# A differential-attention and mixture-of-experts kernel: another order of work within a round, one further GpSimd step per round, and two norms from one set of statistics

## The chip, the cores and the metric

The kernel runs on one core of a Trainium2 chip. A core has five engines with a queue each: TensorE (PE, matmuls; its weight loads are listed apart as PEld), VectorE (DVE), ScalarE (ACT), GpSimd (POOL) and SyncE (SP), which here only issues DMAs. An engine takes its instructions in the order in which they were recorded; between engines there are semaphores. The metric is the time of one execution on the device, in microseconds, as the median of several runs.

## What is computed

One transformer layer on x of 8 sequences, 512 tokens, 128 features (float32). Attention with 16 heads of 8 features subtracts two softmaxes, and the result is normalised by the sum of its absolute values; a layer norm of the residual sum follows. Then each token goes through a second norm with gamma and beta, a router chooses two of eight experts, and the weighted outputs are added and normed again.

```python
attn = softmax(causal(q @ k1.T * SCALE)) - sigmoid(lambda_logit) * softmax(causal(q @ k2.T * SCALE))
attn = attn / maximum(sum(abs(attn)), 1e-6)
x  = layernorm(x + (attn @ v) @ Wo.T)                    # no gamma, no beta
xn = (x - mean(x)) * rsqrt(var(x) + 1e-5) * gamma + beta
w, idx = top_k(softmax((xn @ router_w.T) / 1.5), 2)      # of 8 experts
y  = sum over the two chosen e of w_e * (silu(xn @ W1[e]) @ W2[e])      # 128 -> 512 -> 128
out = layernorm(x + y)
```

## The kernel before

**Tiles.** Queries are taken in 16 units per sequence (class Unit), 32 queries each, with all 16 heads: four heads times 32 queries fill the 128 partitions, and four groups of heads (NG = 4) lie side by side. Unit j needs L = 32 (j + 1) keys. Four units are a block of 128 tokens; there are 4 blocks in a sequence and 32 in all.

**Rounds.** The attention is a pipeline of 384 rounds (function round_of). A unit with L up to 256 has two slots, each with two head groups and both softmaxes; a longer one has four slots, each with two head groups and one softmax. A slot passes through these steps, one engine each:

- scores (PE, L343 and, with the causal mask, L352), into PSUM tile sc, of which there are two buffers
- maxima (DVE, L365 for short units, L373 for long ones), into nm
- exps (ACT, L383), from sc and nm into the unit's tile et, with row sums
- combine (DVE, L395 to L399 once a unit and L409; then POOL, L419), which multiplies the second softmax's numerators in place by -c2; a unit has two pieces (short) or four (long)
- transposes (PE, L437), which turn and subtract both softmaxes of a piece in PSUM tile pt, of which there is one buffer
- evacuate (ACT, L457 and L459), from pt into aT
- times_v (PE, L469), once a unit, into po

Within one call of round_of the order of every engine is the order in which the function records its steps; nothing rearranges it. Before, a call records: times_v of the units that are ready, with the first steps of a finished block; scores of the next slot; evacuate of the pieces that the previous round transposed; the ScalarE steps that the previous round left in a list (on_act); maxima of the present slot; transposes of the pieces that the previous round combined; the VectorE steps left in a list (on_dve); combine; exps of the present slot; late VectorE steps (on_dve_late). Then come one step of a finished block or of the next sequence's projections (misc), one step of routing, one or two DMA steps on GpSimd (moves, gathers), and up to two expert steps as a budget (level, due) allows.

**Around the attention.** block_tasks has seven steps for a finished block: reciprocals, normalise, project_out, first_norm, second_norm, turn, logits; each norm has bn_stats, bn_aggr, an addition of eps on DVE and a power of -0.5 on GpSimd (L112). projection_tasks makes the next sequence's qb (queries spread over four heads by four GpSimd instructions, L292), kT and vt. The 30 first blocks form four chunks of 6, 9, 9 and 6, whose tokens are sorted by expert: route_tasks counts and places them, the queue moves sends rows to DRAM by indirect DMAs on GpSimd (L751), sparse_tasks runs tiles of 128 rows through their expert (turn: L860, L869; hidden: L889; silu: ACT L827 and DVE L829), and the queue gathers fetches rows back (L914). The last two blocks go through all experts (dense_tasks). When the attention is over, round_of is called without a slot until all lists are empty.

## Time and profile before

| what | us |
|---|---|
| median of 3 runs | 1285.85 |
| lowest, highest | 1284.31, 1290.01 |
| the profiled execution, on the device | 1278.93 |
| its span, first to last instruction | 1277.1 |
| mean granted PE clock in it | 0.926 |

The busiest groups of instructions, from the page:

| group | count | busy us | mean ns |
|---|---|---|---|
| transposes (PE, L437) | 2560 | 393.2 | 294 |
| exps, long units (ACT, L383) | 512 | 299.3 | 591 |
| multiplication (POOL, L419) | 512 | 267.7 | 528 |
| combine (DVE, L409) | 512 | 264.0 | 516 |
| maxima, long units (DVE, L373) | 256 | 251.8 | 984 |
| scores, long units (PE, L343) | 1024 | 248.7 | 562 |
| evacuate (ACT, L457) | 336 | 149.3 | 444 |
| power -0.5 (POOL, L112) | 96 | 62.1 | 647 |

A busy time is the union of a group's instructions, so that matmuls that overlap count once; a mean is the length of one. A wait is the idle time of an engine ahead of an instruction, put down to what released it. The granted clock is a share of full speed[...].

### The profile page before, as it was taken

Reading aid. Unit: us, or ns where it says so; the run is one execution under the profiler, and the core shown is the slowest. Engines: PE = TensorE matmul, PEld = TensorE weight load, DVE = VectorE, ACT = ScalarE, POOL = GpSimd, SP = SyncE. Lnnn points to the kernel's source line nnn. Section 1 sums busy time; section 2 is a strip of 40 time slices with the busy share of each in tenths; the row PEclk is TensorE's granted clock in tenths of the full one; section 3 lists DMA queues with packets and bytes.
Section 4 is the critical chain, followed back from the end, with each engine's and each line's share of the span. In section 5 each row is a group of like instructions: output and inputs, shape, how many; then the busy total and the mean of one; then the engine's idle time right before and its main releaser. Section 6 shows DMA issues by size and latency. Waiting matters only on the chain.

```text
span 1277.1 us, 30618 instructions
## 1 busy us (share of the span) xinstructions
PE 1152.4 (90%) x10538; PEld 844.4 (66%) x10538; DVE 947.2 (74%) x2900; ACT 804.3 (63%) x2912; POOL 502.6 (39%) x867
## 2 busy tenths in 40 slices
PE   5999999889999999998999999998998699879776
PEld 3666666567666766675657776785667587657665
DVE  3588768877887878986796888688777776747656
ACT  3677767666786767776656767775665465636321
POOL 3243334452423333366373332324546531244343
PEclk8599969897999999999889999999899798979998
DMA  8000000021100310020212321141023334223762
GB/s 236 1 2 2 10 1 2 26 73 51 41 22 22 92 43 22 11 83 26 61 48 69 93 63 42 43 113 48 26 72 87 111 107 114 79 66 112 224 184 66
DMA packets 115594, 82.87 MB, mean 65 GB/s; under 512 B 9584, under 2 KB 100976, under 8 KB 115440
## 3 DMA queue, kind: packets, MB, share of 16 engines
q1 hardware_dynamic: 97632, 66.67, 18.3%
q0 software_dynamic: 3840, 7.87, 2.1%
q10 hardware_dynamic: 13968, 6.37, 1.8%
q8 instruction: 85, 1.39, 0.5%
q14 instruction: 69, 0.57, 0.2%
HBM read 63.31 MB, written 17.56 MB: 63 GB/s over the span
## 4 chain that ended last, share of the span: by engine, by line
PE 64%; DVE 17%; ACT 7%; POOL 6%; issue 5%; DMA 2%; ACTq 0%; SPq 0%; POOLq 0%; DVEq 0%
PE pt L437 21%; PE sc L343 13%; PE sc_None L343 6%; PE po L469 6%; PE pa L869 5%; PE pz L889 4%; ACT et L383 4%; DVE junk L409 3%; DVE nm L373 3%; PE pmo L520 2%; DVE hT L829 1%; DVE x L924 1%; POOL l_rs L112 1%; DVE nm L365 1%; POOL et L419 1%
## 5 line engine op out<-in xcount | busy, mean ns | idle before, releaser
L419 POOL TENSOR_SCALAR et<-et,c 128x224 f32<-128x224 f32 (+15 forms) x512 | 267.7, 528 | 491.6 <-DVE junk L409 349.0
L437 PE MATMUL pt<-ident,et 128*128 128x128 f32 (+3 forms) x2560 | 393.2, 294 | 48.3 <-POOL et L419 32.4
L437 PEld LDWEIGHTS pt<-ident,et 128*128 128x128 f32 (+3 forms) x2560 | 277.6, 138 | 170.5 <-issue 45.0
L383 ACT ACTIVATE et<-sc,nm 128x512 f32<-128x512 f32 (+7 forms) x512 | 299.3, 591 | 45.0 <-DVE nm L373 31.7
L373 DVE TENSOR_REDUCE nm<-sc 128x2 f32<-128x576 f32 (+7 forms) x256 | 251.8, 984 | 60.8 <-PE sc L352 59.8
L409 DVE SCALAR_TENSOR_TENSOR junk<-et,c 128x224 f32<-128x224 f32 (+15 forms) x512 | 264.0, 516 | 9.6
L343 PE MATMUL sc<-kT,qb 32*128 32x384 f32 (+7 forms) x1024 | 248.7, 562 | 6.4 <-ACT et L383 5.6
L457 ACT COPY aT<-pt 128x256 f32<-128x256 f32 (+1 forms) x336 | 149.3, 444 | 152.7 <-PE pt L437 149.0
L383 ACT ACTIVATE et<-sc_None,nm 128x256 f32<-128x256 f32 (+7 forms) x512 | 187.2, 378 | 28.4 <-DVE nm L365 13.7
L343 PE MATMUL sc_None<-kT,qb 32*128 32x128 f32 (+7 forms) x1024 | 134.4, 377 | 9.7 <-ACT et L383 9.1
L343 PEld LDWEIGHTS sc<-kT,qb 32*128 32x128 f32 x1024 | 78.9, 188 | 61.3 <-issue 25.5
L365 DVE TENSOR_REDUCE nm<-sc_None 128x4 f32<-128x256 f32 (+7 forms) x128 | 95.8, 749 | 29.7 <-PE sc_None L352 29.5
L343 PEld LDWEIGHTS sc_None<-kT,qb 32*128 32x128 f32 x1024 | 86.0, 208 | 43.5 <-ACT et L383 16.7
L112 POOL TENSOR_TENSOR l_rs<-l_ve,nhalf 128x1 f32<-128x1 f32 x96 | 62.1, 647 | 125.0 <-DVE l_ve L110 99.5
L469 PE MATMUL po<-aT,vt 128*32 128x128 f32 (+3 forms) x2560 | 107.9, 288 | 0.0
L889 PE MATMUL pz<-xgT,w 128*128 128x128 f32 x704 | 99.9, 288 | 6.8 <-DVE xgT L863 3.6
L869 PE MATMUL pa<-w,hT 128*128 128x128 f32 x704 | 98.2, 285 | 7.0 <-DVE hT L829 4.3
L383 ACT ACTIVATION_READ_ACCUMULATOR et<-sc_None,nm 128x1 f32 x512 | 104.2, 203 | 0.0
L383 ACT ACTIVATION_READ_ACCUMULATOR et<-sc,nm 128x1 f32 x512 | 102.0, 199 | 0.0
L869 PEld LDWEIGHTS pa<-w,hT 128*128 128x128 f32 x704 | 91.2, 202 | 9.4 <-DVE hT L829 6.7
L889 PEld LDWEIGHTS pz<-xgT,w 128*128 128x128 f32 x704 | 91.4, 202 | 8.9 <-DVE xgT L863 4.3
L459 ACT COPY aT<-pt 32x128 f32<-32x128 f32 (+5 forms) x288 | 84.6, 294 | 7.6 <-PE pt L437 7.6
(143 smaller groups left out, 1290.3 us busy)
## 6 DMA issues: line engine op xcount, KB each, us to landing
w<-in_w_dram SPq DMA_DIRECT2D x192, 256.0 KB, 3.0
xg<-xs SPq DMA_DIRECT2D x88, 64.0 KB, 3.3
ys<-ysb ACTq DMA_DIRECT2D x88, 64.0 KB, 1.6
xs<-zero SPq DMA_DIRECT2D x2, 1600.0 KB, 13.4
xs<-zero SPq DMA_DIRECT2D x2, 1216.0 KB
xt<-in_x_dram SPq DMA_DIRECT2D x8, 256.0 KB, 2.9
out_dram<-ot SPq DMA_DIRECT2D x32, 64.0 KB, 1.5
xs<-xh,row POOLq DMA_INDIRECT x60, 2.3
```

The lines of the kernel that those rows point to most:

```text
L343: nc.tensor.matmul(sc[:, gi, lo : lo + L], lhsT=qb[r, j].rearrange("p h q -> p (h q)"), rhs=kT[r, si, :L], start=True, stop=False,)
L365: nc.vector.tensor_reduce(self.nm[:, g, :], sc.rearrange("p g (s l) -> p g s l", s=2)[:, :, :, : self.L], AX.X, ALU.max, negate=True,)
L373: nc.vector.tensor_reduce(self.nm[:, g, s], sc[:, :, : self.L], AX.X, ALU.max, negate=True)
L383: nc.scalar.activation(self.et[:, g, si, : self.L], sc[:, gi, lo : lo + self.L], AF.Exp, bias=self.nm[:, g, si : si + 1], accum_out=self.b ...
L409: nc.vector.scalar_tensor_tensor(junk[:, :L], self.et[:, g, 1, :L], self.c2[:, g : g + 1], self.et[:, g, 0, :L], ALU.mult, ALU.max, accum_ ...
L419: nc.gpsimd.tensor_scalar(self.et[:, g, 1, :L], self.et[:, g, 1, :L], self.c2[:, g : g + 1], -1.0, ALU.mult, ALU.mult,)
L437: nc.tensor.matmul(pt[:kw, x_ * self.n + kb, :], lhsT=self.et[:, g, k, kb * P : kb * P + kw], rhs=ident, is_transpose=True, start=(k == 0) ...
L457: nc.scalar.copy(self.aT[:, g, :full, :], src[:, :, :full, :])
L459: nc.scalar.copy(self.aT[: w[-1], g, full, :], src[: w[-1], :, full, :])
L469: nc.tensor.matmul(self.blk["po"][32 * g : 32 * g + 32, self.jj, :], lhsT=vt[:kw, kb, 32 * g : 32 * g + 32], rhs=self.aT[:kw, g, kb, :], s ...
L869: nc.tensor.matmul(pm[:, 1, :], lhsT=hT[y][:, f, :], rhs=w[y][1][:, f, :], start=(f == 0), stop=(f == NF - 1),)
L889: nc.tensor.matmul(pz[:, f, :], lhsT=w[t][0][:, f * P : (f + 1) * P], rhs=xgT[t], start=True, stop=True,)
```

## The change

round_of records its steps in another order. At the start it sets aside the pieces that are to be transposed and the units that are to be multiplied with v. Then: scores of the next slot, maxima of the present slot, combine, on_act, exps, on_dve, on_dve_late; then misc, **or** a step of routing if misc is empty; GpSimd's step; experts; and at the end evacuate of what the previous round transposed, times_v, and the transposes.

GpSimd's step is taken from a new list on_pool first, which holds the four spreads of the queries one by one; then from moves; then from gathers, but these only in a round that had neither misc nor routing.

The two norms become one step. The second norm normalises what the first one put out, so its mean is 0 and its variance v / (v + eps); from the first norm's variance v, residual makes v + eps and v (1 + eps) + eps^2, takes both to the power -0.5 in one GpSimd instruction, and norms writes xh and x1, both from xa. Three small tiles that outlast their chunk's routing (w1st, w2nd, row) get a third buffer.

```diff
@@ -286,17 +286,19 @@
                 pm = ps_m.tile([P, T], F32, tag="pm", name=f"pmq_{b}")
                 nc.tensor.matmul(pm, lhsT=wq_sb, rhs=xTf, start=True, stop=True)
 
+                def spread_head(h):
+                    nc.gpsimd.tensor_scalar(
+                        qb[:, :, h, :],
+                        qs.rearrange("p (j q) -> p j q", q=Q),
+                        hms[:, h : h + 1],
+                        1.0,
+                        ALU.mult,
+                        ALU.mult,
+                    )
+
                 def spread():
                     nc.vector.tensor_copy(qs, pm)
-                    for h in range(4):
-                        nc.gpsimd.tensor_scalar(
-                            qb[:, :, h, :],
-                            qs.rearrange("p (j q) -> p j q", q=Q),
-                            hms[:, h : h + 1],
-                            1.0,
-                            ALU.mult,
-                            ALU.mult,
-                        )
+                    on_pool.extend(lambda h=h: spread_head(h) for h in range(4))
 
                 on_dve.append(spread)
 
@@ -530,31 +532,36 @@
                     nc.vector.tensor_add(xa, pm, xts[b][:, i, :])
                     mv = bp.tile([P, 1, 2], F32, tag="mv1", name=f"mv1_{n}")
                     stats_of(bp, xa, mv[:, 0, :], "l1")
-                    s["xa"], s["mv"], s["rs"] = xa, mv, rstd_of(bp, mv, 1, "l1")
+
+
+
+                    ve = bp.tile([P, 2], F32, tag="l1_ve", name=f"l1_ve_{n}")
+                    nc.vector.tensor_scalar(ve[:, 0:1], mv[:, 0, 1:2], EPS, None, ALU.add)
+                    nc.vector.tensor_scalar(
+                        ve[:, 1:2], mv[:, 0, 1:2], 1.0 + EPS, EPS * EPS, ALU.mult, ALU.add
+                    )
+                    rs = bp.tile([P, 2], F32, tag="l1_rs", name=f"l1_rs_{n}")
+                    nc.gpsimd.tensor_tensor(rs, ve, nhalf[:, :2], ALU.pow)
+                    s["xa"], s["mv"], s["rs"] = xa, mv, rs
 
                 on_dve.append(residual)
 
-            def first_norm():
+            def norms():
                 def norm():
-                    x1 = s["x1"] = ch.x1[:, ci, :]
-                    nc.vector.tensor_scalar(
-                        x1, s["xa"], s["mv"][:, 0, 0:1], s["rs"], ALU.subtract, ALU.mult
-                    )
-                    mv = bp.tile([P, 1, 2], F32, tag="mv2", name=f"mv2_{n}")
-                    stats_of(bp, x1, mv[:, 0, :], "l2")
-                    s["mv2"], s["rs2"] = mv, rstd_of(bp, mv, 1, "l2")
-
-                on_dve.append(norm)
-
-            def second_norm():
-                def norm():
+                    x1 = ch.x1[:, ci, :]
                     if ch.sparse:
                         s["xh"] = ch.xh[:, ci, :]
                     else:
                         s["xh"] = bp.tile([P, D], F32, tag="xh", name=f"xh_{n}")
-                    nc.vector.tensor_scalar(
-                        s["xh"], s["x1"], s["mv2"][:, 0, 0:1], s["rs2"], ALU.subtract, ALU.mult
-                    )
+                    for k, dst in enumerate((s["xh"], x1)):
+                        nc.vector.tensor_scalar(
+                            dst,
+                            s["xa"],
+                            s["mv"][:, 0, 0:1],
+                            s["rs"][:, 1 - k : 2 - k],
+                            ALU.subtract,
+                            ALU.mult,
+                        )
 
                 on_dve.append(norm)
 
@@ -574,7 +581,7 @@
                 nc.tensor.matmul(pm, lhsT=s["xnT"], rhs=rw_sb, start=True, stop=True)
                 on_dve.append(lambda: nc.vector.tensor_copy(lg[:, ci, :], pm))
 
-            return [reciprocals, normalise, project_out, first_norm, second_norm, turn, logits]
+            return [reciprocals, normalise, project_out, norms, turn, logits]
 
         def route_tasks(ch):
 
@@ -648,8 +655,8 @@
                         nc.vector.tensor_mul(e2, r["ex"], r["oh2"])
                         m = small("s2")
                         nc.vector.tensor_reduce(m, e2, AX.X, ALU.add)
-                        ch.w = [r["rc"], cp.tile([P, CB], F32, tag="w2nd", name=f"w2nd_{n0}")[:, :nb]]
-                        ch.w[0] = cp.tile([P, CB], F32, tag="w1st", name=f"w1st_{n0}")[:, :nb]
+                        ch.w = [r["rc"], x1p.tile([P, CB], F32, tag="w2nd", name=f"w2nd_{n0}")[:, :nb]]
+                        ch.w[0] = x1p.tile([P, CB], F32, tag="w1st", name=f"w1st_{n0}")[:, :nb]
                         nc.vector.tensor_copy(ch.w[0], r["rc"])
                         nc.vector.tensor_mul(ch.w[1], m, r["rc"])
                     else:
@@ -722,7 +729,7 @@
                         pk = wide(f"p{k}")
                         nc.vector.tensor_mul(pk, at, r[f"oh{k + 1}"])
                         nc.vector.tensor_reduce(pos[:, k], pk, AX.X, ALU.add)
-                    ch.row = cp.tile([P, 2, CB], U32, tag="row", name=f"row_{n0}")
+                    ch.row = x1p.tile([P, 2, CB], U32, tag="row", name=f"row_{n0}")
                     nc.vector.tensor_copy(ch.row[:, :, :nb], pos)
 
                 on_dve.append(step)
@@ -1020,7 +1027,7 @@
             return tasks + [lambda c=c: on_dve.append(lambda: last[c][1]()) for c in range(nb)]
 
 
-        on_act, on_dve, on_dve_late = [], [], []
+        on_act, on_dve, on_dve_late, on_pool = [], [], [], deque()
 
         def pause():
             pass
@@ -1035,6 +1042,7 @@
             task()
             run(on_dve)
             run(on_act)
+            run(on_pool)
 
         misc, routing, experts, moves, gathers = (deque() for _ in range(5))
         to_combine, to_transpose, to_evacuate, to_multiply = deque(), deque(), deque(), deque()
@@ -1076,46 +1084,44 @@
 
 
             nonlocal due, now_at
-            for _ in range(len(to_multiply)):
-                after_blocks(to_multiply.popleft())
+            to_turn, to_times = list(to_transpose), list(to_multiply)
+            to_transpose.clear()
+            to_multiply.clear()
             if ahead:
                 ahead["sc"] = ahead["u"].scores(ahead["slot"])
-            for _ in range(len(to_evacuate)):
-                v, piece, pt = to_evacuate.popleft()
-                v.evacuate(piece, pt)
-                if piece[-1] == NG - 1:
-                    to_multiply.append(v)
-            run(on_act)
             if now:
                 now["u"].maxima(now["slot"], now["sc"])
-            for _ in range(len(to_transpose)):
-                v, piece = to_transpose.popleft()
-                to_evacuate.append((v, piece, v.transposes(piece)))
-            run(on_dve)
             left = now["left"] if now else 2
             for _ in range(-(-len(to_combine) // left)):
                 v, piece = to_combine.popleft()
                 v.combine(piece)
                 to_transpose.append((v, piece))
+            run(on_act)
             if now:
                 now["u"].exps(now["slot"], now["sc"])
                 if now["left"] == 1:
                     to_combine.extend((now["u"], piece) for piece in now["u"].pieces)
+            run(on_dve)
             run(on_dve_late)
-            room = 2
+            room, busy = 2, True
             if misc:
                 misc.popleft()()
                 room -= 1
-            if routing:
+            elif routing:
                 step = routing.popleft()
                 step()
                 room -= step.__name__ == "counts"
+            else:
+                busy = False
+
 
 
             for _ in range(1 if now and now["u"].b < B - 1 else 2):
-                if moves:
+                if on_pool:
+                    on_pool.popleft()()
+                elif moves:
                     moves.popleft()()
-                elif gathers and (now or not misc and not routing):
+                elif gathers and not busy:
                     gathers.popleft()()
             if now:
                 t, c = rounds[now_at]
@@ -1128,6 +1134,15 @@
                 due -= 1
                 room -= 1
             due = min(due, 4.0)
+            for _ in range(len(to_evacuate)):
+                v, piece, pt = to_evacuate.popleft()
+                v.evacuate(piece, pt)
+                if piece[-1] == NG - 1:
+                    to_multiply.append(v)
+            for v in to_times:
+                after_blocks(v)
+            for v, piece in to_turn:
+                to_evacuate.append((v, piece, v.transposes(piece)))
 
...
@@ -1163,7 +1178,7 @@
             attention_done = True
             while (
                 to_combine or to_transpose or to_evacuate or to_multiply
-                or misc or routing or experts or moves or gathers or on_act or on_dve or on_dve_late
+                or misc or routing or experts or moves or gathers or on_act or on_dve or on_dve_late or on_pool
             ):
                 round_of()
```

## The prediction

> **What bounds the kernel now.** I read the page's engine line and its chain of waits first, then PE's waits between 40 and 1165 us (attention without its start and drain), then one quiet stretch of the timeline, then the granted clock by windows of 10 us.
>
> ```profile
> PE 1152.4 (90%) x10538; PEld 844.4 (66%) x10538; DVE 947.2 (74%) x2900; ACT 804.3 (63%) x2912; POOL 502.6 (39%) x867
> PE 64%; DVE 17%; ACT 7%; POOL 6%; issue 5%; DMA 2%; ACTq 0%; SPq 0%; POOLq 0%; DVEq 0%
> ```
>
> TensorE is busy 90% and is 64% of the chain; 125 us of the span are left for it to be idle, and about 60 of these lie in the start and the drain. What it waits for in between:
>
> ```profile
> PE pt L437 <- POOL et L419: 32.4, 24, 4.4
> PE pt L437 <- ACT aT L457: 9.9, 14, 0.8
> PE sc_None L343 <- ACT et L383: 7.2, 17, 1.1
> PE pa L860 <- DVE hT L829: 7.1, 9, 3.8
> PE sc L343 <- ACT et L383: 5.6, 15, 0.9
> ```
>
> (waiting instruction, releaser, us in total, times, longest). The transposes wait 32.4 us for GpSimd's multiplication. The new order bears most on this. Now a round with nothing but attention in it, L = 416:
>
> ```profile
> 102.20 0.97 PE L343 MATMUL sc<-kT,qb 32*128 32x416 f32 x4
> 103.01 0.18 PE L352 MATMUL sc<-mk,i 32*128 32x32 bf16 x2
> 103.12 0.87 PE L437 MATMUL pt<-ident,et 128*128 128x128 f32 x6
> 103.37 1.02 DVE L373 TENSOR_REDUCE nm<-sc 128x2 f32<-128x832 f32 x1
> 104.03 0.37 ACT L457 COPY aT<-pt 128x256 f32<-128x256 f32 x1
> 104.30 0.27 ACT L459 COPY aT<-pt 96x128 f32<-96x128 f32 x1
> 104.46 0.61 ACT L383 ACTIVATE et<-sc,nm 128x416 f32<-128x416 f32 x1
> 105.05 0.60 ACT L383 ACTIVATE et<-sc,nm 128x416 f32<-128x416 f32 x1
> ```
>
> (start, duration). PE goes from scores to transposes to the next scores (103.97) without a gap: 1.77 us a round. ScalarE evacuates pt **before** this round's exponentials, so pt is free when the next transposes come. Last, the clock:
>
> ```profile
> 100.00:110.00 10.00, 9.96 (x89) 5.94 (x86) 8.42 (x19) 8.43 (x28) 2.90 (x5) 1.00 0.01 2
> 160.00:170.00 10.00, 9.29 (x59) 6.90 (x59) 7.54 (x30) 6.38 (x31) 3.65 (x9) 0.53 0.01 2
> 170.00:180.00 10.00, 10.00 (x57) 6.92 (x58) 5.45 (x19) 6.16 (x26) 2.47 (x5) 0.50 0.00 0
> 300.00:310.00 10.00, 9.60 (x62) 7.01 (x56) 7.48 (x28) 5.29 (x24) 3.42 (x9) 0.53 0.19 61
> 1180.00:1190.00 10.00, 6.67 (x63) 6.17 (x65) 6.62 (x23) 2.43 (x6) 6.79 (x8) 1.00 0.63 181
> ```
>
> (after the length: busy us of PE, weight load, DVE, ACT, POOL, then the granted clock.) The mean clock of 0.926 is (1 - 0.926) x 2 x 1277 = 189 us at half speed, in stretches of 5 to 30 us. PE is then saturated, so up to 94 us are lost there.
>
> **The change, part by part.**
>
> *Transposes to the end of PE's round.* They get the time of the misc and expert matmuls (about 1 us where there are any) as slack for GpSimd, and the multiplication itself is issued earlier, since combine now stands ahead of on_dve. The waits of 1.15 to 1.32 us at L = 320 (80, 204, 238, 339, 468 us) should go: 6 us. Of the other 26 (3.1 and 4.4 us at 1114 and 1125, where two sends a round keep GpSimd for some 5 us, which stays so) I take half. Sum **-19**.
>
> *Exponentials ahead of the evacuation on ScalarE.* Scores wait for them 7.2 + 5.6 us now: **-13**. But pt has one buffer. In the changed instruction order the scores wait for VectorE alone, and the transposes carry the wait for ScalarE: transposes of round r need the evacuation of r-1, which now stands behind exps of r, which need maxima of r, which need scores of r, which stand behind the transposes of r-2. That is a loop over two rounds. From the rows above: scores 0.99, maxima 1.02, exps 2 x 0.61, evacuation 0.55 (mean of one copy of 0.48 and two of 0.63), transposes 0.87, three hand-overs of about 0.06: 4.84 us for two rounds, 9.7 for a unit of four. Measured now: 7.8 (100.38 to 108.20). So PE must wait 1.9 us in this unit. The same sum for L = 352, 384, 448, 480, 512 gives 9.1, 9.5, 10.1, 10.9, 11.3; the first batch has 8.7, 7.8, 9.2, 10.4, 9.7. With 416 it falls short by 7.0 us. Over the eight batches, from the starts of the scores: 7.0, 3.5, 5.4, 4.6, 3.5, 2.3, 0.5, 0: **+27**. This is a lower end, since matmuls of one round don't fill the wait of another, and a tanh that waits for its matmuls delays exps in the loop (1.06 + 0.60 in place of 1.02): 0 to 30, I take **+15**. Units up to L = 256 take 6 to 10 us and stay above their loop.
>
> *DVE and ScalarE steps behind the attention's.* on_dve waits for the previous round's matmuls, which now come before transposes, so it stalls less; what hides it is the slack of a round. PE's expert waits (7.1, and 5.6 in smaller rows) fall by **-4**. If on_dve is late, maxima of the next round queue behind it, as now.
>
> *Norms.* Per block a stats, an aggregate and a pow go (295 + 182 ns on DVE, 647 on GpSimd), one DVE add of about 154 comes: 32 x 0.32 = 10 us of DVE, 21 us of GpSimd, beside PE's work nearly everywhere: 0 to -10, I take **-2**. Where DVE is not the bound it buys nothing. The pow on two columns costs as the one does now, within 0.1 us: nothing on the path.
>
> *One thing a round on GpSimd; misc or routing.* The four head spreads (733 ns each, 2.9 us in a row at 598.61) are parted over four rounds, counted above in the first 6 us. They go ahead of sends; the queries have over ten rounds until used. Gathers keep off rounds with misc or routing. Routing of the third chunk's count moves from round 303 to 319, so its experts begin later and 58 instead of 56 expert steps are left behind the last scores; the drain takes 108 us for 56: **+4**. Weight loads on SP go with these steps, in the same order. The row and weight tiles with a third buffer cost nothing and free nothing that was waited for.
>
> *The clock.* Stretches at half clock follow stalls on GpSimd at 240, 467, 600, 657, 884, 934, 1005 and 1113, together some 118 us, at a loss of up to 59. With the waits partly gone I take **-25** (0 to -50). Against it stand the new waits. [...] the widest gap ahead of the half clock at 160 was 0.94 us, ahead of 300 1.12, and of ten single gaps of 0.9 to 1.5 us about half are followed by it. At 1180 the clock is full with PE busy only 67%, so idleness alone doesn't decide. [...] Then scores, 51% of a plain round now (0.92 of 1.77), fall to 38% (of 2.42), near the 34% of the rounds before 160 (0.95 of 2.8). A plain round at half clock is about 3.7 us instead of 2.4 (3.9 and 4.5 measured at 662, L = 512). Some 30 units are plain, 120 rounds; none cold is 0, half 78, a quarter **+40**, which I take[...].
>
> Sum: -19 -13 +27 +15 -4 -2 +4 -25 +40 = **+23**. The profiled execution took 1278.9, its span 1277.1: 1302. The median shown is 7 us above it; I say **1304**.
>
> **Rivals.** (1) *Faster*: waits on GpSimd and their half clock go as hoped, no new half clock, the loop costs its lower end alone: -63 + 27 + 4 = -32, **1247**. For it speaks that the plain loss is small; against it, that PE would have to stay warm with a gap in each plain round. It decides once the extra of the loop and new half clock stay under 32 us. (2) *Worse*: PE is cold in most plain rounds and the old half-clock stretches remain: +23 + 38 + 25 = **1365**. For it: 160 and 300, cold with PE busy 93% and more; against it, that cold PE is saturated[...]. (3) *Cancelling*: 15 us of new half clock instead of 40 gives about **1281 to 1290**, within what can be told. (4) The order isn't what it says, because a queue or a buffer undoes it: the built order shows transposes behind the experts and combine right after maxima, so this falls.
>
> **How the numbers follow.** Slower by the loop and some half clock 0.42, cold throughout 0.14, cancelling 0.13, faster 0.31. Faster and slower by 0.5% are below 1279.4 and above 1292.3, about what a measurement tells from no change. So 0.31, 0.13, 0.56. The range 1240 to 1372 leaves a tenth at each end; the likeliest case alone is 1293 to 1340.
>
> **What would show it.** Right: PE's transposes wait for aT (evacuation) some 40 us or more instead of 13; hardly any wait of scores for et; plain units at 416 take near 9.7 us; mean clock not above 0.92. Wrong: those units still 7.8 us, or a clock of 0.95 and more with GpSimd's waits gone.

## The result, and the profile after

| what | before | after |
|---|---|---|
| median, us | 1285.08 | 1367.07 |
| lowest, highest | 1283.67, 1290.01 | 1366.49, 1378.36 |
| profiled execution, us | 1278.93 | 1366.49 |
| mean granted PE clock | 0.926 | 0.892 |

The ratio is 1.065 (95% interval 1.059 to 1.071): **slower**, by 82 us in the medians and 88 in the profiled executions, where the prediction had 23. The sign is as forecast and the time lies in the range, but it is the time of rival 2 (1365), which had been given a chance of 0.14. Here and below, medians are over all executions and ratios over the fast ones alone.

The engine line and the chain that ended last, from the page of the changed kernel:

```profile
PE 1220.1 (89%) x10538; PEld 867.5 (64%) x10538; DVE 943.3 (69%) x2836; ACT 796.5 (58%) x2912; POOL 482.8 (35%) x835
PE 61%; DVE 21%; ACT 8%; issue 4%; DMA 3%; POOL 2%; SPq 0%; ACTq 0%; POOLq 0%; DVEq 0%
```

TensorE has exactly as many matmuls as before (10538) and is busy 68 us longer with them; its idle time in the span goes from 125 to 145 us. GpSimd's share of the chain falls from 6% to 2%, and VectorE's rises from 17% to 21%: the wait that the change aims at is nearly gone from the chain, and another has come. The attention's stage alone, from 40 us to just behind its last scores, in one window of each kernel (from:to, length, then the busy us of PE, weight load, DVE, ACT and POOL, the granted clock, the DMAs' share, GB/s). Before:

```profile
40.00:1166.00 1126.00, 1047.35 (x9734) 755.51 (x9733) 863.33 (x2626) 757.05 (x2774) 446.58 (x721) 0.93 0.18 51
```

After:

```profile
40.00:1247.00 1207.00, 1108.38 (x9682) 772.78 (x9674) 854.51 (x2547) 747.88 (x2767) 422.94 (x684) 0.89 0.16 47
```

This stage has 81 of the 88 us: 61 are busy time, 20 are idle time (78.6 to 98.6). (52 fewer matmuls fall into the stage than before, and 45 more behind it.) The other engines do less than before. So the loss is mostly a slower TensorE, not a TensorE that waits longer. Its waits in that stage, by releaser, in the changed kernel:

```profile
PE pt L439 <- ACT aT L461: 34.3, 48, 1.9
PE pt L439 <- ACT aT L459: 22.7, 25, 1.4
PE pmo L522 <- DVE on L512: 7.8, 18, 1.6
...
PE pmn L570 <- DVE xh L557: 3.1, 6, 1.0
PE pt L439 <- POOL et L421: 2.4, 1, 2.4
```

(L439, L459, L461 and L421 are the transposes, the two evacuations and GpSimd's multiplication.) The transposes' wait for GpSimd has gone from 32.4 to 2.4 us, that of the scores for the exponentials from 12.8 to nothing, and in their place the transposes wait 57.0 us for the evacuation. This is the loop through the single buffer pt. One turn of it in a plain round, on the timeline:

```profile
542.21 0.57 ACT L385 ACTIVATE et<-sc,nm 128x384 f32<-128x384 f32 x1
...
542.77 0.37 ACT L459 COPY aT<-pt 128x256 f32<-128x256 f32 x1
...
543.02 0.26 ACT L461 COPY aT<-pt 64x128 f32<-64x128 f32 x1
...
543.34 0.87 PE L439 MATMUL pt<-ident,et 128*128 128x128 f32 x6 [0.94 <-ACT aT L461]
```

ScalarE finishes the exponentials, then empties pt, and only then do the transposes start, after TensorE has been idle for 0.94 us. What such a gap can be followed by shows a few rounds later:

```profile
552.53 0.87 PE L439 MATMUL pt<-ident,et 128*128 128x128 f32 x6 [1.13 <-ACT aT L461]
553.33 0.97 PE L345 MATMUL sc<-kT,qb 32*128 32x416 f32 x4
...
554.42 1.54 PE L439 MATMUL pt<-ident,et 128*128 128x128 f32 x6
```

The same six transposes take 0.87 us at 552.53, behind a gap of 1.13 us, and 1.54 us in the next round. In the first sequence the windows show how long that lasts:

```profile
100.00:110.00 10.00, 9.09 (x50) 5.14 (x50) 4.91 (x14) 6.03 (x23) 2.19 (x4) 0.69 0.01 2
110.00:120.00 10.00, 10.00 (x59) 5.89 (x58) 4.99 (x12) 4.37 (x15) 1.38 (x3) 0.50 0.00 0
```

Before, the first of these windows had 89 matmuls at a clock of 1.00; now it has 50 at 0.69, and the second runs wholly at half clock with TensorE busy all of it. In the traces of both kernels the clock is either 1 or 0.5, so half speed rules for (1 - 0.892) x 2 x 1364.8 = 295 us of the span, against 189 before.

How full TensorE is ahead of such a stretch can be counted. In the traces of both kernels all changes of the clock lie on one grid of 3.41 us: its stretches between two changes last from 3.41 to 201.39 us, each a whole multiple of 3.413. These are two neighbouring pieces of the grid, around the rounds above:

```profile
550.94:554.35 3.41, 2.25 (x18) 1.05 (x14) 2.18 (x6) 3.23 (x12) 1.17 (x2) 0.99 0.00 0
554.35:557.77 3.42, 3.35 (x13) 1.97 (x13) 1.62 (x4) 1.67 (x6) 0.58 (x1) 0.50 0.00 0
```

TensorE is busy 2.25 of the 3.41 us (66%), and the next piece is at half clock. Over both kernels, of the pieces at full clock in which TensorE is busy less than half of the time, 17 of 20 are followed by half clock; of those with one half to three quarters, 24 of 76; of those with 80% or more, 2 of 503. In the piece from 550.94 the single wait of 1.13 us is nearly all of TensorE's idle time (1.16 us).

### The profile page after: what moved, and what is told of

Read it like the earlier page. It is cut to its first block, busy times and chain, and to the rows that moved or that the text cites. A ratio compares the mean times of both kernels' runs of the same rounds, so it can differ in the third digit from the quotient of the medians.

```text
span 1364.8 us, 30258 instructions
## 1 busy us (share of the span) xinstructions
PE 1220.1 (89%) x10538; PEld 867.5 (64%) x10538; DVE 943.3 (69%) x2836; ACT 796.5 (58%) x2912; POOL 482.8 (35%) x835
## 4 chain that ended last, share of the span: by engine, by line
PE 61%; DVE 21%; ACT 8%; issue 4%; DMA 3%; POOL 2%; SPq 0%; ACTq 0%; POOLq 0%; DVEq 0%
PE pt L439 18%; PE sc L345 12%; PE po L471 7%; PE sc_None L345 6%; DVE nm L375 6%; ACT et L385 5%; PE pz L896 5%; DVE junk L411 5%; PE pa L876 4%; PE pmo L522 3%; ACT aT L459 1%; DMA got<-ys,row 1%; DVE nm L367 1%; PE pmk L307 1%; DVE x L931 1%
## 5 line engine op out<-in xcount | busy, mean ns | idle before, releaser
L421 POOL TENSOR_SCALAR et<-et,c 128x224 f32<-128x224 f32 (+15 forms) x512 | 270.4, 533 | 710.3 <-DVE junk L411 488.2
L439 PE MATMUL pt<-ident,et 128*128 128x128 f32 (+3 forms) x2560 | 402.8, 302 | 63.5 <-ACT aT L461 34.8
L439 PEld LDWEIGHTS pt<-ident,et 128*128 128x128 f32 (+3 forms) x2560 | 301.9, 145 | 148.7 <-ACT aT L461 73.4
L411 DVE SCALAR_TENSOR_TENSOR junk<-et,c 128x224 f32<-128x224 f32 (+15 forms) x512 | 258.9, 506 | 9.6
L345 PE MATMUL sc<-kT,qb 32*128 32x384 f32 (+7 forms) x1024 | 265.0, 596 | 0.0
L459 ACT COPY aT<-pt 128x256 f32<-128x256 f32 (+1 forms) x336 | 149.6, 445 | 47.3 <-PE pt L439 46.5
L345 PEld LDWEIGHTS sc<-kT,qb 32*128 32x128 f32 x1024 | 83.7, 200 | 59.9 <-issue 43.1
L471 PE MATMUL po<-aT,vt 128*32 128x128 f32 (+3 forms) x2560 | 117.3, 308 | 0.0
L896 PE MATMUL pz<-xgT,w 128*128 128x128 f32 x704 | 106.6, 299 | 5.0 <-DVE xgT L870 5.0
L834 ACT ACTIVATE th<-pz 128x512 f32<-128x512 f32 x88 | 52.7, 599 | 84.7 <-PE pz L896 83.9
L471 PEld LDWEIGHTS po<-aT,vt 128*32 128x32 f32 (+3 forms) x2560 | 66.0, 118 | 43.0 <-issue 33.5
```

The lines of the kernel that those rows point to most:

```text
L345: nc.tensor.matmul(sc[:, gi, lo : lo + L], lhsT=qb[r, j].rearrange("p h q -> p (h q)"), rhs=kT[r, si, :L], start=True, stop=False,)
L411: nc.vector.scalar_tensor_tensor(junk[:, :L], self.et[:, g, 1, :L], self.c2[:, g : g + 1], self.et[:, g, 0, :L], ALU.mult, ALU.max, accum_ ...
L421: nc.gpsimd.tensor_scalar(self.et[:, g, 1, :L], self.et[:, g, 1, :L], self.c2[:, g : g + 1], -1.0, ALU.mult, ALU.mult,)
L439: nc.tensor.matmul(pt[:kw, x_ * self.n + kb, :], lhsT=self.et[:, g, k, kb * P : kb * P + kw], rhs=ident, is_transpose=True, start=(k == 0) ...
L459: nc.scalar.copy(self.aT[:, g, :full, :], src[:, :, :full, :])
L471: nc.tensor.matmul(self.blk["po"][32 * g : 32 * g + 32, self.jj, :], lhsT=vt[:kw, kb, 32 * g : 32 * g + 32], rhs=self.aT[:kw, g, kb, :], s ...
```

## Experiments

Four theories were set against each other. **L**: the loop through pt (exponentials ahead of the evacuation) makes the waits, and the waits make the half clock. **P**: the loss comes from TensorE's new order, with the transposes behind the round's other matmuls. **V** (called D in the first expectations): VectorE's steps of on_dve come too late behind the combine and hold up the matmuls of misc and experts. **R**: it comes from the rules (one thing a round on GpSimd, misc or routing, gathers in empty rounds), which push work later. The kernel before was timed beside each run; ratios are to it, with 95% intervals.

### The changed kernel with the evacuation put back ahead

```diff
+            for _ in range(len(to_evacuate)):
+                v, piece, pt = to_evacuate.popleft()
+                v.evacuate(piece, pt)
...
             run(on_act)
             if now:
```

(and the same lines taken away at the end of round_of).

> The changed kernel with one thing put back: the evacuation of pt stands ahead of on_act and of the exponentials on ScalarE, as before the change; all else is the new order. Theory L (the loop exps, evacuation, transposes, scores, maxima over one pt buffer makes TensorE wait in each plain round, and these waits bring the half clock): the waits of the transposes for aT fall from 58 us to 20 or less, a plain unit at L = 416 goes from 9.5 us and more to 8.3 or less, the mean clock rises to 0.92 or more, and the time is 1215 to 1290 us. Rival R (the parted GpSimd steps, misc or routing, the late gathers and the later experts leave TensorE with too little work in places): the time stays above 1340 us and the clock below 0.90. Rival D (late on_dve steps hold up what follows): above 1320 us with waits for xgT, on, hT in place of those for aT.

Measured: 1357.37 us, ratio 1.058 (1.051 to 1.065). The loop is gone, the shortest units at L = 384, 416, 448 and 512 are back at 8.0, 7.9, 8.4 and 9.8 us, and the time has hardly moved. TensorE's waits in the stage (40 to 1241 us):

```profile
PE sc L345 <- ACT et L385: 16.2, 26, 1.8
PE pmo L522 <- DVE on L512: 15.8, 19, 2.6
PE pmn L570 <- DVE xh L557: 12.1, 15, 1.2
PE sc_None L345 <- ACT et L385: 10.6, 22, 1.1
PE pmc L683 <- DVE r_bothb L676: 10.4, 4, 4.1
```

Theory L alone falls, and the waits for `on` at a time above 1320 us are what theory V (rival D) had forecast. Instead of the transposes, the matmuls of the finished blocks wait now (pmo, pmn) and so do the scores. Why pmo waits is plain on the timeline:

```profile
94.48 0.55 DVE L411 SCALAR_TENSOR_TENSOR junk<-et,c 128x320 f32<-128x320 f32 x1
...
94.96 0.68 DVE L512 TENSOR_TENSOR on<-oraw,pmr 128x512 f32<-128x512 f32 x1
...
95.70 1.16 PE L522 MATMUL pmo<-wo_sb,on 128*128 128x128 f32 x8 [0.49 <-DVE on L512]
```

VectorE takes the combine (L411) first and only then the step that makes `on`; TensorE's pmo, which before stood behind the transposes, is next in line and waits. That suggested that VectorE's new order is a second cause of the same kind, hidden under the first.

### The changed kernel with the combine put back behind on_dve

```diff
-            for _ in range(-(-len(to_combine) // left)):
-                v, piece = to_combine.popleft()
-                v.combine(piece)
-                to_transpose.append((v, piece))
+            pieces = [to_combine.popleft() for _ in range(-(-len(to_combine) // left))]
             run(on_act)
...
             run(on_dve)
+            for v, piece in pieces:
+                v.combine(piece)
+                to_transpose.append((v, piece))
```

> The changed kernel with VectorE's order alone put back: combine behind on_dve; the evacuation stays behind the exponentials and the transposes last. Known by now: with the evacuation alone put back 1357 us, with both put back 1283 us. If VectorE's order is the greater part of the loss, 1285 to 1320 us. If either of the two is enough for most of it (the loop still makes TensorE wait for aT in plain rounds, and the half clock follows), 1325 to 1370 us, with 40 us or more of waits for aT and a mean clock of 0.91 or less.

Measured: 1360.02 us, ratio 1.064 (1.054 to 1.074). No better either: the intervals of the changed kernel and of these two overlap. Here the waits for VectorE are small, and the loop takes 64.7 us in the attention's stage:

```profile
PE pt L439 <- ACT aT L461: 39.0, 60, 1.2
PE pt L439 <- ACT aT L459: 25.7, 26, 2.0
```

### Both put back

> The changed kernel with both put back: evacuation ahead of the exponentials, and combine behind on_dve; the transposes stay last, and the norms and the rules of a round stay as changed. Theory L+V: the loss is gone, 1255 to 1300 us, against 1357 us with the evacuation alone put back. Theory P: 1330 us or more. Theory V: as L+V.

Measured: 1283.16 us, ratio 1.004 (1.000 to 1.008), clock 0.960. So with TensorE's new order, the norms and the rules in place, the two orders make this table (us):

| | combine ahead of on_dve (changed) | combine behind (as before) |
|---|---|---|
| evacuation behind exps (changed) | 1367.07 | 1360.02 |
| evacuation ahead (as before) | 1357.37 | 1283.16 |

**Either order alone costs 74 to 77 us, and both together 84.** The intervals don't tell the 84 from either alone. So the two costs don't add; why one nearly covers the other was not tested. The attention's stage of the three other corners, with the clock behind the five busy times. These are single executions, of 1370, 1336 and 1275 us, which lie 13 above, 24 below and 8 below their medians. Evacuation put back:

```profile
40.00:1241.00 1201.00, 1088.58 (x9673) 766.20 (x9671) 857.37 (x2546) 744.17 (x2764) 422.61 (x683) 0.91 0.16 47
```

Combine put back:

```profile
40.00:1214.00 1174.00, 1086.06 (x9677) 761.75 (x9674) 841.97 (x2545) 745.00 (x2764) 424.10 (x682) 0.91 0.17 48
```

Both put back:

```profile
40.00:1146.00 1106.00, 1022.71 (x9672) 721.47 (x9670) 836.81 (x2542) 742.83 (x2763) 423.65 (x682) 0.97 0.18 51
```

The loop by itself (second row against third) makes this stage 68 us longer: TensorE's idle time grows from 83.3 to 87.9 us, its busy time by 63. VectorE's order by itself (first against third) makes it 95 us longer: 29 idle, 66 busy. The difference between 68 and 95 is partly which executions were profiled, since the medians have 77 and 74. In both cases most is busy time. In the loop's case TensorE is idle for nearly the same sum as without it; what differs is the clock, 0.91 against 0.97.

### Does the half clock cause it, or only go with it? Added work as the test

If TensorE slows because it falls idle for short times, then work that nobody reads, put into those times, must make the kernel faster; if the slow matmuls have another cause, it must make it slower. Eight bf16 matmuls of 128x128 go ahead of the transposes in each attention round in which TensorE has no matmul of a finished block, of the projections or of an expert. Their results are not read. (`did` is set in rounds with such a matmul; these lines are left out here.)

```diff
+            if now and not did:
+                fm = ps_m.tile([P, P], F32, tag="pm", name=f"fill_{now_at}")
+                for _ in range(8):
+                    nc.tensor.matmul(fm, lhsT=before, rhs=ones, start=True, stop=True)
             for v, piece in to_turn:
```

> The changed kernel, with eight more matmuls (128x128x128, bfloat16, results never read) ahead of the transposes in each of the 68 rounds with no other TensorE task[...]. If it is the lack of TensorE work in these rounds that brings the half clock, the mean clock rises from 0.892 to 0.92 or more and the time falls to 1300 to 1345 us although there is more to do. If the half clock has nothing to do with these rounds, the clock stays at 0.89 and the time is 1367 to 1400 us.

Measured, in the changed kernel: 1328.96 us, ratio 1.035 (1.027 to 1.043), clock 0.944 instead of 0.892. By the trace the fillers stand in 137 rounds (where an expectation names another number, this one holds), 0.62 us each at full clock (median); their busy time is 92 us in all, and the kernel is 38 us **shorter**. Its window from 100 to 120 us is at full clock throughout, where the changed kernel had 0.69 and 0.50. In the stage:

```profile
40.00:1218.00 1178.00, 1100.81 (x10753) 791.83 (x10751) 860.35 (x2555) 748.68 (x2781) 423.52 (x686) 0.95 0.17 48
```

1071 matmuls more than the changed kernel, and 8 us less of busy time: the matmuls that count take less, by more than the fillers add. Half speed falls from 295 us to 149 (from the clock, as above).

The same in the kernel with the combine put back, which has the loop as its only cause:

> The changed kernel with combine put back behind on_dve (1360 us) and the eight plain filler matmuls in the 68 rounds. If what is left of the loss there is mostly half clock that the loop's waits bring, the clock rises to 0.94 or more and the time falls to 1285 to 1325 us; if the waits themselves are the loss, 1340 us or more.

Measured: 1308.97 us, ratio 1.021 (1.014 to 1.029), clock 0.952: 51 us less than without the fillers. The transposes' wait for the evacuation falls from 64.7 to 38.6 us:

```profile
PE pt L439 <- ACT aT L459: 21.3, 23, 2.7
PE pt L439 <- ACT aT L461: 17.3, 36, 1.8
```

So of the 77 us that the loop costs, the fillers give back 51.

The third filler run puts transposes, one bf16 128x128 at a time, where the matmuls were:

```diff
+                fm = ps_m.tile([P, P], BF16, tag="pm", name=f"fill_{now_at}")
+                for _ in range(8):
+                    nc.tensor.transpose(fm, before, identb)
```

> As the changed kernel with eight filler matmuls in each of the 68 rounds with no other TensorE task, but the fillers are transposes (matmuls in transpose mode, 128x128, bfloat16, results never read). With plain matmuls the time went from 1367 to 1329 us and the clock from 0.892 to 0.944. If a transpose counts for the clock as a matmul does, again 1320 to 1340 us and 0.93 or more. If it doesn't, the clock stays below 0.91 and the time is 1355 to 1385 us.

Measured: 1335.43 us, ratio 1.038 (1.029 to 1.047), clock 0.945. The interval overlaps that of the matmuls (1.027 to 1.043), and the clock is as high with transposes as with matmuls (0.945 and 0.944).

### The parts alone, from the kernel before

ScalarE's order alone, exponentials ahead of the evacuation; the ScalarE steps of on_act moved behind it too:

```diff
-            for _ in range(len(to_evacuate)):
...
-            run(on_act)
             if now:
                 now["u"].maxima(now["slot"], now["sc"])
...
                     to_combine.extend((now["u"], piece) for piece in now["u"].pieces)
+            for _ in range(len(to_evacuate)):
...
+            run(on_act)
             run(on_dve_late)
```

> The kernel before, with the order of ScalarE alone changed: exponentials, then evacuation, then on_act; transposes stay right behind the scores, nothing else moves. Theory L: the loop is there with none of the rest of the change, so the transposes wait 40 us or more for aT, the clock falls below 0.91 and the time is 1330 to 1390 us. Rival R: ScalarE's order is hidden, the time is within 1 per cent of 1285. Rival D: likewise, since VectorE's order is that of before.

Measured: 1560.62 us, ratio 1.215 (1.206 to 1.225). Theory L's sign, but far beyond its size. TensorE's order is as before here (the transposes are recorded later, in the same place among its work). Its waits over the whole execution:

```profile
PE pt L437 <- ACT aT L459: 142.3, 127, 4.0
PE pt L437 <- ACT aT L457: 45.3, 35, 3.1
```

The transposes wait 187.6 us for the evacuation, and the clock is 0.82: half speed for 567 us. These are the waits and the slow clock of L, and the waits are three times those of the changed kernel (57.0 us). Why they are so long was not tested: the transposes stand right behind the scores here, with nothing to cover the wait, but on_act moves as well.

TensorE's order alone:

```diff
             if ahead:
                 ahead["sc"] = ahead["u"].scores(ahead["slot"])
+            to_turn = list(to_transpose)
+            to_transpose.clear()
...
-            for _ in range(len(to_transpose)):
-                v, piece = to_transpose.popleft()
-                to_evacuate.append((v, piece, v.transposes(piece)))
...
             due = min(due, 4.0)
+            for v, piece in to_turn:
+                to_evacuate.append((v, piece, v.transposes(piece)))
```

> The kernel before, with TensorE's order alone changed: the transposes stand at the end of the round, behind misc and experts; times_v, ScalarE and VectorE as before. Theory P (putting the transposes last is the root: the evacuation then ends late wherever it stands, and the exponentials or the next transposes behind it): 1330 us or more, with ScalarE waiting for the transposes 250 us or more. Theory V (VectorE's combine ahead of on_dve holds up the matmuls of misc and experts): within 2 per cent of 1281. Theory L+V (ScalarE's order and VectorE's order share the loss): within 2 per cent of 1281.

Measured: 1298.65 us, ratio 1.018 (1.009 to 1.027). Theory P has at most a part of the loss, 23 us by this ratio; as sole cause it falls with the 1283 us of both put back, where the transposes are still last.

VectorE's order alone, the combine ahead of on_dve:

```diff
-            run(on_dve)
             left = now["left"] if now else 2
             for _ in range(-(-len(to_combine) // left)):
...
                 to_transpose.append((v, piece))
+            run(on_dve)
```

> The kernel before, with VectorE's order alone changed: combine ahead of on_dve. Theory V: 1330 us or more, with TensorE waiting for on, xh, xgT, hT. Theory P: 1265 to 1295 us, since the matmuls of misc and experts still stand behind the transposes. Theory L+V: 1280 to 1320 us.

Measured: 1275.28 us, ratio 0.994 (0.989 to 0.999). The order that costs 74 us behind TensorE's new order costs nothing with the old one. The difference in the code is that the transposes then stand between the scores and the matmuls that read what on_dve makes; this says that it is the two together that hurt. The run with norms and rules below (1255.95 us) has the combine ahead and the old order of TensorE too, and shows no cost either.

The rules alone (head spreads one by one, misc or routing, gathers in empty rounds, the third buffer):

```diff
-            room = 2
+            room, busy = 2, True
...
-            if routing:
+            elif routing:
...
-                if moves:
+                if on_pool:
+                    on_pool.popleft()()
+                elif moves:
...
-                elif gathers and (now or not misc and not routing):
+                elif gathers and not busy:
```

> The kernel before, with only the rules for what a round takes changed: spreads one by one on GpSimd, misc or routing, gathers only in rounds with neither, and the three tiles with a third buffer. Theory L: no loop, and fewer waits for GpSimd, so 1255 to 1290 us. Rival R: this is where the loss comes from, 1330 us or more.

Measured: 1270.32 us, ratio 0.989 (0.981 to 0.996). Faster: theory R falls.

The norms alone (the diff's residual and norms):

> The kernel before, with only the two norms made one step from one set of statistics. Every theory: 10 us less of VectorE and 21 us less of GpSimd, nearly all beside other work: 1270 to 1285 us.

Measured: 1256.01 us, ratio 0.987 (0.977 to 0.998), clock 0.942. That is 16 us by the ratio where the prediction took 2. The profiled execution (1244 us, the fastest of the four) has (1 - 0.942) x 2 x 1242.6 = 144 us at half speed instead of 189, and TensorE's transposes wait 16.4 us for GpSimd's multiplication instead of 32.4. This points at the pow that GpSimd no longer does; it was not tested apart from VectorE's part.

### What is worth keeping

Norms and rules, with all orders as before:

> The kernel before with the norms and the rules of a round from the change, and none of the new order on any engine. Each alone brought some 1 per cent; if they add, 1235 to 1268 us; if both only take the same waits for GpSimd away, 1255 to 1275 us.

Measured: 1258.64 us, ratio 0.976 (0.964 to 0.988). With the combine ahead as well:

> As the kernel before with norms and rules, and combine ahead of on_dve on VectorE as well, with TensorE's and ScalarE's order as before. Alone this order was worth 0.5 per cent: 1228 to 1265 us if it helps here too. If combine first costs as it does behind the new TensorE order, above 1290 us.

Measured: 1255.95 us, ratio 0.978 (0.971 to 0.986): nothing more, the intervals lie on each other. Norms and rules with eight fillers at the end of rounds of short units (L up to 256) that have no other TensorE task, 34 rounds by the trace:

> The kernel before with the norms and the rules from the change (1259 us), with eight plain filler matmuls in those rounds of units up to L = 256 that have no other TensorE task, where the clock falls in the first three batches. If missing work brings the half clock there too, the clock rises above 0.95 and the time is 1225 to 1252 us; if not, 1255 to 1275 us.

Measured: 1251.53 us, ratio 0.968 (0.958 to 0.979). This is faster than both kernels. It is not told apart from the version without fillers, whose interval it overlaps.

## Why the prediction was right and wrong

**Waits for GpSimd, -19.** Right in kind, too small: they fell by 30 us. The two waits at 1114 and 1125, half of which it left in place, went as well (one of 2.4 us is left in the stage); the last sequence is the only one that became shorter, 186 us instead of 199 from its first scores to the stage's end.

**Scores' wait for the exponentials, -13.** Right.

**The loop, +27 and +15.** Right in mechanism, and near in size as far as units run at full clock. Such units of four rounds take 9.0 us at L = 384 (9.5 forecast), 11.1 at 512 (11.3), 11.7 at 480 (10.9), 9.8 at 352 (9.1), and at 416 in the third sequence 9.5 (9.7). The transposes' waits for the evacuation rose from 13.4 to 57.0 us, where "some 40 us or more" was to show it.

**Steps on VectorE, -4.** Right for the expert matmuls that it names, whose waits for VectorE fell from 10.1 to 4.1 us in the stage. But it left out the matmuls of finished blocks and of routing (pmr, pmo, pmn, pmc, pml): their waits for VectorE and GpSimd rose from 6.7 to 26.5 us. The step said that on_dve stalls less and that a round's slack hides it. Moving the transposes behind these matmuls took that slack away: they stand right behind the scores now, and their inputs come after the combine. The runs make this the second of two sufficient causes, and the prediction has no term for it. These four terms together were to add 6 us of waiting; TensorE's idle time in the stage rose by 20.

**Norms, -2.** Too small, with a measured 16 us (3 to 30 by the interval) when they are the only change. "Where DVE is not the bound it buys nothing" looked at VectorE; the waits that fell were those for GpSimd. The pow on two columns took 709 ns against 647 for one, as forecast.

**Later experts, +4.** Right in sign: the stretch behind the attention grew from 111 to 118 us.

**The clock, -25 and +40.** This is the step that failed, by its size. Net it gave +15 us; half speed grew from 189 to 295 us, and half of the 106 us counts as lost, **+53** (an estimate: the transposes of a group start 213 ns apart at half clock and 109 at full clock). Busy time, with the same matmuls, says +61 in the stage and +68 in the span; the 15 us between 53 and 68 are not accounted for. Two choices made it small. It took a quarter of the plain rounds as being at half clock, +40; by its own figures (120 rounds, 2.4 us or 3.7 at half clock) half of them is 78 us and all 156. But the unit at L = 416, forecast at 9.7 us, took 13.2 to 14.2 in five of the eight sequences, and the first two sequences (117 and 132 us before, 140 and 154 after), in which 56 of the 137 filler rounds lie, went from a clock of 0.85 and 0.88 to 0.73 and 0.77. By the same formula they had 67 us at half speed before and 146 after: 79 of the 106. And it took new half clock as a matter of plain rounds only, so it did not see that VectorE's order makes gaps of the same kind in the others: with the loop taken out, half speed fell only from 295 to 255 us (clock 0.907 in the profiled 1370 us), idle time in the stage rose from 98.6 to 112.4 us, and the median stayed at 1357 us.

In the changed kernel half clock mostly came without a long idle gap: 22 of the 26 stretches at half clock follow a piece of 3.41 us that no idle gap longer than 2.44 us touches. The prediction made plain rounds likely to fall to half clock by the share of the scores alone, 38% of a round against 34% ahead of 160, which leaves the transposes out. That plain rounds fall to half clock came true, but that reason isn't borne out: the fillers that are bf16 transposes brought the clock to 0.945, those that are matmuls to 0.944. What goes with half clock in the traces of the two kernels is the share of a 3.41 us piece in which TensorE is busy, transposes counted (half clock followed 17 of 20, 24 of 76 and 2 of 503 pieces, as above).

**Rivals.** Rival 2 has the measured time, but in part by luck: it kept all the old stretches at half clock and added 78 us, which it called "most plain rounds" but which is the prediction's own figure for half of them. The runs show a net 53 us for the clock instead of 78, and the rest of its sum is made up by the 14 us of idle time that no term had and by busy time that the clock doesn't explain. Its argument against itself, that TensorE is saturated at half clock, doesn't decide: from 110 to 120 us TensorE is busy for 10.00 of the 10 us and stays at 0.50. How much of the old half clock went and how much is new was not parted. Rival 1 falls with the clock, rival 3 with its 15 us of half clock. Rival 4 falls on the trace, where the transposes stand as the order says.

Of the signs that were to show the prediction right, the transposes' wait (57.0 us), the scores' (nothing) and the clock (0.892) came; the unit of 9.7 us at L = 416 came in the third sequence alone (9.5), and half clock lengthened it in five others.

**Left open**: what decides whether half clock follows a badly filled piece of 3.41 us (it followed 41 of the 96 below three quarters), and what ends it; why the waits are so long with the exponentials' order alone on the kernel before; why the costs of the two orders don't add; and how the 26 us of the loop that the fillers leave (77 - 51) are shared between real waits and rounds without fillers. No run tried these. A second buffer for pt, which would cut the loop, was not tried either.

## What to carry to other kernels

Where the trace shows a clock that falls after short waits, cost a reordering by the number and place of the new gaps, not by their sum: here 5 us more of idle time went with 63 us more of busy time. Ask how many short pieces (here of 3.41 us) it leaves less than three quarters full: half clock followed 41 of the 96 such pieces in the two kernels, and 4 of the 525 fuller ones. When steps on several engines are reordered together, take each wait that the old order covered and ask what stands between the two instructions now; one cause can hide behind another of the same size, so put back each alone and both. A few matmuls that nobody reads are a cheap test of whether TensorE is slow for want of work (here 1096 of them took the clock from 0.892 to 0.944 and 38 us off the time), and sometimes worth keeping.

## What the runs showed of the hardware

- In the traces of both kernels the granted clock is 1 or 0.5 and changes on a grid of 3.41 us. Of the pieces at full clock, half clock followed 17 of the 20 with TensorE busy less than half of the time, 24 of the 76 between one half and three quarters, and 2 of the 503 with 80% or more.
- In the changed kernel half clock followed a piece (550.94 to 554.35) in which one idle gap of 1.13 us was nearly all of the idle time (1.16 us): six transposes took 0.87 us at 552.53 and 1.54 us at 554.42.
- A saturated TensorE at half clock did not always get its full clock back at once. In the two kernels 113 pieces at half clock were over 98% busy, and 38 of them were followed by full clock.
- At half clock the transposes of a group started 213 ns apart instead of 109 (medians, in both kernels), while one of them took 425 ns instead of 278 (means, changed kernel): the spacing was 1.95 times as long, one transpose 1.53 times.
- Adding 1096 matmuls with 92 us of busy time made the changed kernel 38 us faster, and the clock went from 0.892 to 0.944; with bf16 transposes in their place it was 0.945.
